# A patch-wise Fourier stage: one product per group in place of two, and a fixed order on three engines

## The chip, the cores and the metric

The kernel runs on one core of one Trainium2 chip. The metric is the device time of one execution in microseconds; the median of three runs before the change is 7702.65 us (7696.43 to 7703.76). Engines are named as in the profile: PE is TensorE (PEld its weight loads), DVE is VectorE, ACT is ScalarE, POOL is GpSimd, SP is SyncE, which here only issues transfers (DMAs).

## The reference

Four layers are applied to an image of 48 channels and 128 x 128 pixels, each on the normalised image and added to it: an attention, a chain of one-dimensional convolutions swept over rows and columns, the patch layer, and a state-space scan. The change lies in the patch layer:

```python
hidden = _conv2d(x, w_hidden, b_hidden)
qkv = _conv2d(hidden, w_dw, b_dw, groups=C6, padding='SAME')
q, k, v = jnp.split(qkv, 3, axis=1)
q_patch = q.reshape(B, C2, hp, wp, PATCH, PATCH)
k_patch = k.reshape(B, C2, hp, wp, PATCH, PATCH)
q_fft = jnp.fft.rfft2(q_patch)
k_fft = jnp.fft.rfft2(k_patch)
out = jnp.fft.irfft2(q_fft * k_fft, s=(PATCH, PATCH))
out = out.reshape(B, C2, H, W)
mu = jnp.mean(out, axis=1, keepdims=True)
var = jnp.var(out, axis=1, keepdims=True)
normed = (out - mu) / jnp.sqrt(var + EPS)
normed = normed * gamma[None, :, None, None] + beta[None, :, None, None]
return _conv2d(v * normed, w_out, b_out)
```

C is 48, C2 is 96, C6 is 288, PATCH is 8. The reshape to patches takes 64 consecutive pixels of a row as one patch of 8 x 8, so a row of 128 pixels holds two patches. Each patch of q is convolved circularly with that of k, the result is normalised over its 96 channels, gated by v, and taken back to 48 channels.

## The kernel before

The four layers run one after the other. `patch_conv` (L696 to L892) works on 32 groups of G = 4 image rows, with pixels on the partitions and channels along the free axis, all in float32. PE does a float32 product as two instructions, so a product in the code is two records in the profile.

The stages of a group:

- `fill` (L759, eight rows, so two groups) writes the normalised rows into the padded image `xp` (the profile's xa; DVE, L93; POOL sets a row of ones, L761), copies 49 channels one row up to partitions 64 and on (L764), fills the partitions that are left with pieces of further taps (L767, two transfers), and puts what does not fit into one of three tiles `rest` (L777, six transfers of 19 partitions x 1038 elements). All nine transfers of a fill are issued by SP. The first three of the six serve even rows, the others odd rows.
- `convolve` (L782, half a group at a time) makes the 3 x 3 convolution of two rows: three products a row over 128 partitions ("columns", L795, tile pc), then one over the 57 partitions of `rest` ("remainder", L804), and ACT copies pc to qkv (L812).
- `keys` and `queries` take the Fourier transform by products with the table `fm` (L821, tile f). f has one PSUM buffer of two banks. Of the keys ACT makes two copies, kn (L836) and kx with real and imaginary part exchanged (two instructions, L839). Of the queries DVE multiplies both with f (L845, twice).
- `back` takes the inverse transform of the two products with the table `gm`, adding them up in PSUM (L852, tile po, kn then kx). DVE takes the mean and subtracts it (L860 to L863), ACT squares (L865), DVE sums (L867), ACT takes the root (L869), DVE divides (L870, L871), and POOL applies gamma, beta and v (L872 to L874).
- `turn` transposes y on PE (L881) and ACT copies it (L883). `leave` makes the last product (L887); DVE adds it to the image (L891) and takes statistics for the next layer (L892).

The groups are pipelined by hand in the loop at the end of `patch_conv`: iteration g holds the convolution of group g, keys and queries of g-1, back of g-2, and turn and leave of g-3, and a fill ahead of them in every second iteration.

The text is put in an order for each engine by a scheduler, which may move instructions of the text past each other where no dependency forbids it. A call through `InOrder` (L32) instead adds to each instruction a dependency on the one before it through the same object, with no semaphore, so that this engine keeps to the order of the text. In the profile all instructions that are issued through `InOrder` carry the helper's line, L48. Before the change `patch_conv` has no such order. Transfers issued by SP and by ACT signal on eight semaphores that are used in turn, and one that takes a semaphore again waits for the transfer that had it before; so no more than eight are open at once.

After the stage, `image_out` (L1525) stores the image for the scan in eight transfers on SP (L1531), and the scan begins.

Of the kernel before, what the change touches and what calls it, by code (L numbers as in the profile page):

```python
# [26 lines left out]
C = 48  # L27
# [668 lines left out]
def patch_conv(ctx, tc, xq, other, const, ins):  # L696

    nc = tc.nc
    ident = const["ident"]
# [21 lines left out]
    gm = wp.tile([128, 2, 64], F32, name="gm")  # L721
    nc.sync.dma_start(gm.rearrange("p f n -> p (f n)"), ins["c_gm"])
# [36 lines left out]
    def fill(r):  # L759
        inside = xp[0:64, 1 + r : 1 + RN + r, 1 : W + 1]  # L760
        nc.gpsimd.memset(inside[32:64], 1.0)  # L761
        normalise(nc, inside[0:C], rows(xq[0:C, r * W : (r + RN) * W]), stats)
        new = slice(r + 1, r + 1 + RN)
        nc.sync.dma_start(xp[64 : 64 + K1, r : r + RN, :], xp[0:K1, new, :])  # L764
        lo, hi = max(r - 1, 0), H if r + RN == H else r - 1 + RN
        for n in range(2):
            nc.sync.dma_start(  # L767
                xp[64 * n + K1 : 64 * n + 64, lo:hi, :],
                xp[M * n : M * n + M, lo + 2 : hi + 2, :],
            )  # L770
        e = rests[r // RN % 3].rearrange("c h w -> c (h w)")
        size = KR // 3
        long = RN * SP - 2
        for n in range(2):
            for dx in range(3):
                at = 64 * n + size * dx
                nc.sync.dma_start(  # L777
                    e[at : at + size, 0:long],
                    flat[2 * M : K1, (r + 1) * SP + dx : (r + 1) * SP + dx + long],
                )  # L780

    qkv, ks, prod, ys, yts = {}, {}, {}, {}, {}  # L782

    def convolve(g, half):

        if half == 0:
            qkv[g] = vp.tile([128, G, C6], F32, name="qkv")
        r0 = g * G + 2 * half  # L790
        pc = [ps_c.tile([128, C6], F32, name="pc") for _ in range(2)]
        last = r0 + 2 == H
        for i in range(2):
            for dx in range(3):
                nc.tensor.matmul(  # L795
                    pc[i],
                    lhsT=xp[:, r0 + i, dx : dx + W],
                    rhs=wt[:, dx, :],
                    start=(dx == 0),
                    stop=(dx == 2 and i == 1 and last),  # L800
                )
        for i in range(1 if last else 2):
            at = 64 * i
            nc.tensor.matmul(  # L804
                pc[i],
                lhsT=rest(r0 + i)[at : at + KR],
                rhs=wt[at : at + KR, 3, :],
                start=False,
                stop=True,
            )  # L810
        for i in range(2):
            nc.scalar.copy(qkv[g][:, 2 * half + i, :], pc[i])  # L812

    def dft(g, at):


        p = ps_f.tile([128, 2, CH], F32, name="f")
        for patch in range(2):
            here = slice(64 * patch, 64 * patch + 64)
            for part in range(2):  # L820
                nc.tensor.matmul(  # L821
                    p[64 * part : 64 * part + 64, patch, 0 : G * C2].rearrange(
                        "f (r c) -> f r c", c=C2
                    ),
                    lhsT=fm[here, part, :],
                    rhs=qkv[g][here, :, at : at + C2],
                    start=True,
                    stop=True,
                )
        return p[:, :, 0 : G * C2]  # L830

    def keys(g):

        p = dft(g, C2)
        ks[g] = [sp.tile([128, 2, G * C2], F32, name=n) for n in ("kn", "kx")]
        nc.scalar.copy(ks[g][0], p)  # L836
        for part in range(2):
            here, there = (slice(64 * n, 64 * n + 64) for n in (part, 1 - part))
            nc.scalar.copy(ks[g][1][here], p[there])  # L839

    def queries(g):
        p = dft(g, 0)
        prod[g] = ks.pop(g)
        for k in prod[g]:
            nc.vector.tensor_mul(k, p, k)  # L845

    def back(g):

        po = ps_o.tile([128, G, C2], F32, name="po")
        for i, t in enumerate(prod.pop(g)):  # L850
            for patch in range(2):
                nc.tensor.matmul(  # L852
                    po[64 * patch : 64 * patch + 64].rearrange("p r c -> p (r c)"),
                    lhsT=gm[:, i, :],
                    rhs=t[:, patch],
                    start=(i == 0),
                    stop=(i == 1),
                )
        mu = sp.tile([128, G], F32, name="mu")
        nc.vector.tensor_reduce(mu, po, AX.X, ALU.add)  # L860
        nc.vector.tensor_scalar_mul(mu, mu, 1.0 / C2)
        y = sp.tile([128, G, C2], F32, name="y")
        nc.vector.tensor_sub(y, po, over_channels(mu))  # L863
        sq = sp.tile([128, G, C2], F32, name="sq")
        nc.scalar.activation(sq, y, AF.Square)  # L865
        var = sp.tile([128, G], F32, name="var")
        nc.vector.tensor_reduce(var, sq, AX.X, ALU.add)  # L867
        nc.vector.tensor_scalar(var, var, 1.0 / C2, 1e-5, ALU.mult, ALU.add)
        nc.scalar.activation(var, var, AF.Sqrt)  # L869
        nc.vector.reciprocal(var, var)  # L870
        nc.vector.tensor_mul(y, y, over_channels(var))  # L871
        nc.gpsimd.tensor_mul(y, y, over_rows(gamma))  # L872
        nc.gpsimd.tensor_add(y, y, over_rows(beta))
        nc.gpsimd.tensor_mul(y, y, qkv.pop(g)[:, :, 2 * C2 :])  # L874
        ys[g] = y

    def turn(g):
        y = ys.pop(g)
        pt = ps_o.tile([C2, G, 128], F32, name="po")
        for r in range(G):  # L880
            nc.tensor.transpose(pt[:, r, :], y[:, r, :], ident)  # L881
        yts[g] = sp.tile([C2, G, 128], F32, name="yt")
        nc.scalar.copy(yts[g], pt)  # L883

    def leave(g):
        pw = ps_o.tile([C, CH], F32, name="po")
        nc.tensor.matmul(  # L887
# [650 lines left out]
def constants():  # L1538
# [7 lines left out]
    p, f = np.arange(64), np.arange(40)  # L1546
    turn = 2.0 * np.pi / 8.0 * (np.outer(p // 8, f // 5) + np.outer(p % 8, f % 5))
    weight = np.where((f % 5 == 0) | (f % 5 == 4), 1.0, 2.0) / 64.0
    fm = np.zeros((2, 64, 2, 64))
    fm[:, :, 0, :40] = np.cos(turn)  # L1550
    fm[:, :, 1, :40] = -np.sin(turn)
    gm = np.zeros((2, 64, 2, 64))
    gm[0, :40, 0] = (np.cos(turn) * weight).T
    gm[1, :40, 0] = -gm[0, :40, 0]
    gm[:, :40, 1] = (-np.sin(turn) * weight).T
# [7 lines left out]
        "c_gm": gm.reshape(128, 128),  # L1563
# [135 lines left out]
```

## Time and profile before

| what | value |
|---|---|
| median of three runs | 7702.65 us |
| the profiled execution | 7707.8 us, of which span 7706.0 us |
| PE busy, whole span | 6227.8 us (81%) |
| the patch stage, 4514 to 4961 us: PE, DVE, ACT, POOL busy | 404.13, 194.29, 161.83, 97.28 of 447 us |
| mean granted PE clock in the stage | 0.94 of full |
| first columns of the stage | 4523.09 us |
| start of the scan's part after 4961 us: PE, DVE, POOL busy | 1472.89, 2603.67, 2578.60 of 2745 us |

Times in the profile count from the start of the span. A line of the timeline gives start, busy time, engine, line of the code, operation, the tile written and the tiles read, partitions x columns, the shape and the number of instructions merged, and in brackets the idle time before it and what ended it. A line by stretches gives, for each engine, the busy time and the number of instructions, then the granted PE clock, the mean busy share of the core's 16 DMA engines, and the GB/s that they moved. The records of PE overlap, since matmuls are pipelined, so the distance between two starts tells the price of one, not the duration listed.

### The profile page before, as it was taken

Reading aid. Unit: us, or ns where it says so; the run is one execution under the profiler, and the core shown is the slowest. Engines: PE = TensorE matmul, PEld = TensorE weight load, DVE = VectorE, ACT = ScalarE, POOL = GpSimd, SP = SyncE. Lnnn points to the kernel's source line nnn. Section 1 sums busy time; section 2 is a strip of 40 time slices with the busy share of each in tenths; the row PEclk is TensorE's granted clock in tenths of the full one; section 3 lists DMA queues with packets and bytes.
Section 4 is the critical chain, followed back from the end, with each engine's and each line's share of the span. In section 5 each row is a group of like instructions: output and inputs, shape, how many; then the busy total and the mean of one; then the engine's idle time right before and its main releaser. Section 6 shows DMA issues by size and latency. Waiting matters only on the chain. (4 is left out here: it accounts for less than half of the span.)

```text
span 7706.0 us, 203399 instructions
## 1 busy us (share of the span) xinstructions
PE 6227.8 (81%) x93872; PEld 3159.4 (41%) x93872; DVE 3377.0 (44%) x2467; ACT 4455.4 (58%) x4928; POOL 2793.0 (36%) x573
## 2 busy tenths in 40 slices
PE   7999999999999999999888889745545554554555
PEld 2333333333333333333377755334434343434444
DVE  8300000000000000000022234489999999999998
ACT  2566666666666666666624014366666666666665
POOL 1000000000000000000000122289999999999998
PEclk9999999999999999999999999867767767676676
DMA  5000000000000000000000011166556656666775
GB/s 76 10 3 3 3 2 3 3 3 2 3 3 3 2 3 3 2 3 3 6 1 17 1 31 48 23 166 166 158 160 161 157 161 154 163 157 161 180 180 148
DMA packets 167597, 488.84 MB, mean 63 GB/s; under 512 B 33440, under 2 KB 51968, under 8 KB 163984
## 3 DMA queue, kind: packets, MB, share of 16 engines
q1 hardware_dynamic: 160704, 470.30, 24.3%
q8 instruction: 737, 12.08, 0.7%
q10 hardware_dynamic: 6032, 5.44, 0.3%
q14 instruction: 124, 1.02, 0.0%
HBM read 428.86 MB, written 22.02 MB: 59 GB/s over the span
## 5 line engine op out<-in xcount | busy, mean ns | idle before, releaser
L48 ACT ACTIVATE e<-s,absT 128x1024 f32<-128x1024 f32 x2048 | 2277.3, 1114 | 1217.9 <-PE s L48 1217.9
L1459 POOL TENSOR_TENSOR h<-du,bt 128x3072 f32<-128x3072 f32 (+1 forms) x386 | 2559.5, 6666 | 102.7 <-DMA du<-rep 70.2
L48 PE MATMUL s<-xa,xb 49*64 49x512 f32 x16384 | 2128.4, 589 | 10.6 <-DVE xb L266 10.6
L48 PE MATMUL acc<-e,xb 64*64 64x512 f32 x16384 | 2125.0, 588 | 0.0
L1466 DVE TENSOR_TENSOR_SCAN h<-dA,carry,h 128x1024 f32<-128x1024 f32 x864 | 1940.7, 2329 | 48.9 <-ACT dA L48 32.9
L48 ACT ACTIVATE dA<-dt,a 128x1024 f32<-128x1024 f32 x1152 | 1287.2, 1118 | 864.0 <-DVE h L1466 854.5
L48 PE MATMUL y<-h,cw 128*32 128x48 f32 x49152 | 899.2, 246 | 949.0 <-issue 511.9
L361 DVE TENSOR_TENSOR osum<-o 128x512 f32<-128x512 f32 x32 | 22.2, 692 | 3114.8 <-ACT o L48 3114.8
L593 POOL MEMSET xa<- 48x128 f32 x1 | 0.3, 326 | 3561.0 <-PE acc L48 3561.0
L48 PEld LDWEIGHTS y<-h,cw 128*32 128x32 f32 x49152 | 809.9, 140 | 1072.3 <-issue 661.8
L48 PEld LDWEIGHTS s<-xa,xb 49*64 49x64 f32 x16384 | 626.3, 132 | 1151.2 <-issue 615.6
L48 PEld LDWEIGHTS acc<-e,xb 64*64 64x64 f32 x16384 | 628.6, 132 | 1133.7 <-issue 1111.2
L1466 DVE TENSOR_TENSOR_SCAN h<-dA,h 128x1024 f32<-128x1024 f32 x288 | 636.1, 2272 | 44.1 <-ACT dA L48 33.6
L48 PE MATMUL yz<-ev,sel 128*8 128x48 f32 x4096 | 192.9, 260 | 277.2 <-ACT ev L48 273.3
L48 PEld LDWEIGHTS yz<-ev,sel 128*8 128x8 f32 x4096 | 162.5, 106 | 334.9 <-ACT ev L48 308.7
L657 PE MATMUL p<-xb,w 112*112 112x129 f32 x1524 | 235.7, 291 | 42.2 <-DVE xb L48 42.1
L657 PE MATMUL p<-xa,w 112*112 112x129 f32 x1524 | 233.5, 289 | 41.8 <-DVE xa L48 41.8
L678 POOL TENSOR_TENSOR xb<-xb,xa 48x2048 f32<-48x2048 f32 (+2 forms) x10 | 44.6, 4464 | 563.0 <-DVE xa L48 563.0
L657 PEld LDWEIGHTS p<-xb,w 112*112 112x112 f32 x1524 | 183.7, 178 | 93.9 <-DVE xb L48 93.9
L640 ACT COPY xa<-xb 48x128 f32<-48x128 f32 x256 | 107.4, 419 | 196.6 <-issue 138.1
L657 PEld LDWEIGHTS p<-xa,w 112*112 112x112 f32 x1524 | 181.8, 177 | 93.3 <-DVE xa L48 93.3
L369 DVE RECIPROCAL rec<-y 48x512 f32<-48x512 f32 x32 | 107.1, 3348 | 257.5 <-ACT y L48 257.5
(187 smaller groups left out, 3602.4 us busy)
## 6 DMA issues: line engine op xcount, KB each, us to landing
du<-rep SPq DMA_DIRECT2D x768, 256.0 KB
dt<-rep SPq DMA_DIRECT2D x768, 256.0 KB
rest<-xa SPq DMA_DIRECT2D x96, 77.0 KB
rest<-band SPq DMA_DIRECT2D x48, 129.9 KB
rep<-dd SPq DMA_DIRECT2D x24, 192.0 KB
yd<-ys ACTq DMA_DIRECT2D x256, 12.0 KB
band<-band SPq DMA_DIRECT2D x8, 414.4 KB
xa<-xa SPq DMA_DIRECT2D x16, 199.1 KB
```

The source lines that it names most:

```text
L48: ins = method(*args, **kwargs).ins
L361: nc.vector.tensor_add(self.o, o[:, 0], o[:, 1])
L369: nc.vector.reciprocal(rec, y[64 : 64 + C])
L593: nc.gpsimd.memset(b[64:K, lines, E + W - 1 : E + W], 0.0)
L640: nc.scalar.copy(u[at : at + C, :, y], t[0:C, E + h, E : E + W])
L657: nc.tensor.matmul(p, lhsT=w[0:K, which, i, :], rhs=state[0:K, 2 * i : 2 * i + L], start=False, stop=(i == 2),)
L678: nc.gpsimd.tensor_add(xr, xr, u[0:C, x : x + xr.shape[2], E : E + H].rearrange("c w h -> c h w"),)
L1459: nc.gpsimd.tensor_mul(h[:, p, ks], du.unsqueeze(1).to_broadcast([128, ks.stop - ks.start, LC]), r["bt"][:, ks],)
L1466: nc.vector.tensor_tensor_scan(h[:, p, k, :], dA, h[:, p, k, :], carry[:, i, k : k + 1] if ci else 0.0, ALU.mult, ALU.add,)
```

## The change

It has five parts.

1. The transforms of a patch are packed into 64 real numbers (30 pairs and four that are real by themselves; before, 40 real and 40 imaginary parts of which some repeat). `fm` now holds two forms, one with the halves exchanged. Keys are transformed once with both forms, on the two halves of the partitions, and queries twice with the first, so one product of 128 partitions takes the place of kn and kx. ACT makes one copy of the keys, DVE one multiplication, and `back` has two products (four records) instead of four.
2. `convolve` is split: `columns` makes all twelve products over 128 partitions of a group, `others` the four remainders and the four copies. Between them stands the `turn` of an older group.
3. PE, ACT and DVE issue through `InOrder`, so they follow the text: columns g, turn g-3, others g, keys g-1, back g-2, leave g-3, queries g-1.
4. `back` ends with the square; the rest of the normalisation and the gating is `gate`, placed after `leave`, and ahead of the queries' product and of the image's statistics (`count`) on DVE.
5. The six `rest` transfers of the first fill are issued by ACT instead of SP; the later fills are written at the end of an iteration instead of the start.

```diff
--- before.py
+++ after.py
@@ -696,6 +696,7 @@
 def patch_conv(ctx, tc, xq, other, const, ins):
 
     nc = tc.nc
+    act, pe, dve = (InOrder(tc, e) for e in (nc.scalar, nc.tensor, nc.vector))
     ident = const["ident"]
     C2, C6 = 2 * C, 6 * C
     G = 4
@@ -718,8 +719,8 @@
 
     fm = wp.tile([128, 2, 64], F32, name="fm")
     nc.sync.dma_start(fm.rearrange("p f n -> p (f n)"), ins["c_fm"])
-    gm = wp.tile([128, 2, 64], F32, name="gm")
-    nc.sync.dma_start(gm.rearrange("p f n -> p (f n)"), ins["c_gm"])
+    gm = wp.tile([128, 64], F32, name="gm")
+    nc.sync.dma_start(gm, ins["c_gm"])
     gamma = wp.tile([128, C2], F32, name="gamma")
     nc.scalar.dma_start(gamma, ins["l2_gamma"].to_broadcast([128, C2]))
     beta = wp.tile([128, C2], F32, name="beta")
@@ -756,7 +757,7 @@
 
         return rests[(y + 1) // RN % 3][:, (y + 1) % RN, 0:W]
 
-    def fill(r):
+    def fill(r, queue=nc.sync):
         inside = xp[0:64, 1 + r : 1 + RN + r, 1 : W + 1]
         nc.gpsimd.memset(inside[32:64], 1.0)
         normalise(nc, inside[0:C], rows(xq[0:C, r * W : (r + RN) * W]), stats)
@@ -774,55 +775,60 @@
         for n in range(2):
             for dx in range(3):
                 at = 64 * n + size * dx
-                nc.sync.dma_start(
+                queue.dma_start(
                     e[at : at + size, 0:long],
                     flat[2 * M : K1, (r + 1) * SP + dx : (r + 1) * SP + dx + long],
                 )
 
-    qkv, ks, prod, ys, yts = {}, {}, {}, {}, {}
-
-    def convolve(g, half):
-
-
-
-        if half == 0:
-            qkv[g] = vp.tile([128, G, C6], F32, name="qkv")
-        r0 = g * G + 2 * half
-        pc = [ps_c.tile([128, C6], F32, name="pc") for _ in range(2)]
-        last = r0 + 2 == H
-        for i in range(2):
+    pcs, qkv, prod, lns, ys, yts = {}, {}, {}, {}, {}, {}
+
+    def columns(g):
+
+
+
+        pcs[g] = [ps_c.tile([128, C6], F32, name="pc") for _ in range(G)]
+        for i, pc in enumerate(pcs[g]):
             for dx in range(3):
-                nc.tensor.matmul(
-                    pc[i],
-                    lhsT=xp[:, r0 + i, dx : dx + W],
+                pe.matmul(
+                    pc,
+                    lhsT=xp[:, g * G + i, dx : dx + W],
                     rhs=wt[:, dx, :],
                     start=(dx == 0),
-                    stop=(dx == 2 and i == 1 and last),
+                    stop=(dx == 2 and outside(g, i)),
                 )
-        for i in range(1 if last else 2):
-            at = 64 * i
-            nc.tensor.matmul(
-                pc[i],
-                lhsT=rest(r0 + i)[at : at + KR],
-                rhs=wt[at : at + KR, 3, :],
-                start=False,
-                stop=True,
-            )
-        for i in range(2):
-            nc.scalar.copy(qkv[g][:, 2 * half + i, :], pc[i])
-
-    def dft(g, at):
+
+    def outside(g, i):
+
+        return g * G + i + 1 == H
+
+    def others(g):
+
+        qkv[g] = vp.tile([128, G, C6], F32, name="qkv")
+        for i, pc in enumerate(pcs[g]):
+            at = 64 * (i % 2)
+            if not outside(g, i):
+                pe.matmul(
+                    pc,
+                    lhsT=rest(g * G + i)[at : at + KR],
+                    rhs=wt[at : at + KR, 3, :],
+                    start=False,
+                    stop=True,
+                )
+        for i, pc in enumerate(pcs.pop(g)):
+            act.copy(qkv[g][:, i, :], pc)
+
+    def dft(g, at, forms):
 
 
         p = ps_f.tile([128, 2, CH], F32, name="f")
         for patch in range(2):
             here = slice(64 * patch, 64 * patch + 64)
-            for part in range(2):
-                nc.tensor.matmul(
-                    p[64 * part : 64 * part + 64, patch, 0 : G * C2].rearrange(
+            for n, form in enumerate(forms):
+                pe.matmul(
+                    p[64 * n : 64 * n + 64, patch, 0 : G * C2].rearrange(
                         "f (r c) -> f r c", c=C2
                     ),
-                    lhsT=fm[here, part, :],
+                    lhsT=fm[here, form, :],
                     rhs=qkv[g][here, :, at : at + C2],
                     start=True,
                     stop=True,
@@ -831,44 +837,43 @@
 
     def keys(g):
 
-        p = dft(g, C2)
-        ks[g] = [sp.tile([128, 2, G * C2], F32, name=n) for n in ("kn", "kx")]
-        nc.scalar.copy(ks[g][0], p)
-        for part in range(2):
-            here, there = (slice(64 * n, 64 * n + 64) for n in (part, 1 - part))
-            nc.scalar.copy(ks[g][1][here], p[there])
+        p = dft(g, C2, (0, 1))
+        prod[g] = sp.tile([128, 2, G * C2], F32, name="k")
+        act.copy(prod[g], p)
 
     def queries(g):
-        p = dft(g, 0)
-        prod[g] = ks.pop(g)
-        for k in prod[g]:
-            nc.vector.tensor_mul(k, p, k)
+        p = dft(g, 0, (0, 0))
+        dve.tensor_mul(prod[g], p, prod[g])
 
     def back(g):
 
         po = ps_o.tile([128, G, C2], F32, name="po")
-        for i, t in enumerate(prod.pop(g)):
-            for patch in range(2):
-                nc.tensor.matmul(
-                    po[64 * patch : 64 * patch + 64].rearrange("p r c -> p (r c)"),
-                    lhsT=gm[:, i, :],
-                    rhs=t[:, patch],
-                    start=(i == 0),
-                    stop=(i == 1),
-                )
+        t = prod.pop(g)
+        for patch in range(2):
+            pe.matmul(
+                po[64 * patch : 64 * patch + 64].rearrange("p r c -> p (r c)"),
+                lhsT=gm,
+                rhs=t[:, patch],
+                start=True,
+                stop=True,
+            )
         mu = sp.tile([128, G], F32, name="mu")
-        nc.vector.tensor_reduce(mu, po, AX.X, ALU.add)
-        nc.vector.tensor_scalar_mul(mu, mu, 1.0 / C2)
+        dve.tensor_reduce(mu, po, AX.X, ALU.add)
+        dve.tensor_scalar_mul(mu, mu, 1.0 / C2)
         y = sp.tile([128, G, C2], F32, name="y")
-        nc.vector.tensor_sub(y, po, over_channels(mu))
+        dve.tensor_sub(y, po, over_channels(mu))
         sq = sp.tile([128, G, C2], F32, name="sq")
-        nc.scalar.activation(sq, y, AF.Square)
+        act.activation(sq, y, AF.Square)
+        lns[g] = y, sq
+
+    def gate(g):
+        y, sq = lns.pop(g)
         var = sp.tile([128, G], F32, name="var")
-        nc.vector.tensor_reduce(var, sq, AX.X, ALU.add)
-        nc.vector.tensor_scalar(var, var, 1.0 / C2, 1e-5, ALU.mult, ALU.add)
-        nc.scalar.activation(var, var, AF.Sqrt)
-        nc.vector.reciprocal(var, var)
-        nc.vector.tensor_mul(y, y, over_channels(var))
+        dve.tensor_reduce(var, sq, AX.X, ALU.add)
+        dve.tensor_scalar(var, var, 1.0 / C2, 1e-5, ALU.mult, ALU.add)
+        act.activation(var, var, AF.Sqrt)
+        dve.reciprocal(var, var)
+        dve.tensor_mul(y, y, over_channels(var))
         nc.gpsimd.tensor_mul(y, y, over_rows(gamma))
         nc.gpsimd.tensor_add(y, y, over_rows(beta))
         nc.gpsimd.tensor_mul(y, y, qkv.pop(g)[:, :, 2 * C2 :])
@@ -878,39 +883,46 @@
         y = ys.pop(g)
         pt = ps_o.tile([C2, G, 128], F32, name="po")
         for r in range(G):
-            nc.tensor.transpose(pt[:, r, :], y[:, r, :], ident)
+            pe.transpose(pt[:, r, :], y[:, r, :], ident)
         yts[g] = sp.tile([C2, G, 128], F32, name="yt")
-        nc.scalar.copy(yts[g], pt)
+        act.copy(yts[g], pt)
 
     def leave(g):
         pw = ps_o.tile([C, CH], F32, name="po")
-        nc.tensor.matmul(
+        pe.matmul(
             pw, lhsT=wout, rhs=yts.pop(g).rearrange("c r w -> c (r w)"), start=True, stop=True
         )
         xc = xq[0:C, g * CH : (g + 1) * CH]
-        nc.vector.scalar_tensor_tensor(xc, pw, bout, xc, ALU.add, ALU.add)
-        nc.vector.bn_stats(const["st"][:, g, :], xc)
+        dve.scalar_tensor_tensor(xc, pw, bout, xc, ALU.add, ALU.add)
+
+    def count(g):
+        dve.bn_stats(const["st"][:, g, :], xq[0:C, g * CH : (g + 1) * CH])
 
     NG = H // G
-    fill(0)
+    fill(0, act)
     fill(RN)
     for g in range(NG + 3):
-        if g % (RN // G) == 0 and (g // (RN // G) + 2) * RN < H:
-            fill((g // (RN // G) + 2) * RN)
+
         if g < NG:
-            convolve(g, 0)
+            columns(g)
+        if g >= 3:
+            turn(g - 3)
+        if g < NG:
+            others(g)
         if 0 <= g - 1 < NG:
             keys(g - 1)
-        if g < NG:
-            convolve(g, 1)
-        if g >= 3:
-            turn(g - 3)
-        if 0 <= g - 1 < NG:
-            queries(g - 1)
         if 0 <= g - 2 < NG:
             back(g - 2)
         if g >= 3:
             leave(g - 3)
+        if 0 <= g - 2 < NG:
+            gate(g - 2)
+        if 0 <= g - 1 < NG:
+            queries(g - 1)
+        if g >= 3:
+            count(g - 3)
+        if g % (RN // G) == 0 and (g // (RN // G) + 2) * RN < H:
+            fill((g // (RN // G) + 2) * RN)
@@ -1543,24 +1555,29 @@
-    p, f = np.arange(64), np.arange(40)
...
-    gm = np.zeros((2, 64, 2, 64))
...
+    rows_, cols_ = np.divmod(np.arange(64), 8)
+    once = [(0, 0), (0, 4), (4, 0), (4, 4)]
+    twice = [(a, b) for b in (1, 2, 3) for a in range(8)] + [(a, b) for b in (0, 4) for a in (1, 2, 3)]
...
+    fm[:, :, 0, 0:30] = np.cos(turn[:30]).T
+    fm[:, :, 0, 32:62] = -np.sin(turn[:30]).T
+    fm[:, :, 0, [30, 31, 62, 63]] = np.cos(turn[30:]).T
+    fm[:, :, 1, :32], fm[:, :, 1, 32:] = fm[:, :, 0, 32:], fm[:, :, 0, :32]
+    gm = np.zeros((2, 64, 64))
...
-        "c_gm": gm.reshape(128, 128),
+        "c_gm": gm.reshape(128, 64),
```

More of the change, by code (lines that the diff above doesn't have):

```diff
@@ L1542, in constants @@
     blk[:64, :64] = blk[64:, 64:] = 1.0
-    p, f = np.arange(64), np.arange(40)
-    turn = 2.0 * np.pi / 8.0 * (np.outer(p // 8, f // 5) + np.outer(p % 8, f % 5))
-    weight = np.where((f % 5 == 0) | (f % 5 == 4), 1.0, 2.0) / 64.0
-    fm = np.zeros((2, 64, 2, 64))
-    fm[:, :, 0, :40] = np.cos(turn)
-    fm[:, :, 1, :40] = -np.sin(turn)
-    gm = np.zeros((2, 64, 2, 64))
-    gm[0, :40, 0] = (np.cos(turn) * weight).T
-    gm[1, :40, 0] = -gm[0, :40, 0]
-    gm[:, :40, 1] = (-np.sin(turn) * weight).T
+    rows_, cols_ = np.divmod(np.arange(64), 8)
+    once = [(0, 0), (0, 4), (4, 0), (4, 4)]
+    twice = [(a, b) for b in (1, 2, 3) for a in range(8)] + [(a, b) for b in (0, 4) for a in (1, 2, 3)]
+    angle = 2.0 * np.pi / 8.0
+    turn = angle * np.array([a * rows_ + b * cols_ for a, b in twice + once])
+    fm = np.zeros((2, 64, 2, 64))
+    fm[:, :, 0, 0:30] = np.cos(turn[:30]).T
[3 more added lines that the diff above has]
+    gm = np.zeros((2, 64, 64))
+    gm[0, 0:30] = 2.0 / 64.0 * np.cos(turn[:30])
+    gm[0, 32:62] = -gm[0, 0:30]
+    gm[0, [30, 31, 62, 63]] = np.cos(turn[30:]) / 64.0
+    gm[1, 0:30] = gm[1, 32:62] = -2.0 / 64.0 * np.sin(turn[:30])
     tables = {
```

## The prediction

> **What bounds the kernel now.** I read the page first, to place the stage that is edited; then the busy time by stretches; then PE's timeline of one group of image rows in the steady part; then the start and the end of the stage.
>
> ```profile
> span 7706.0 us, 203399 instructions
> ...
> PE   7999999999999999999888889745545554554555
> ```
>
> A slice is 192.65 us. The patch stage runs from 4514 to 4961 us, slices 23 to 25. The scan after it, 2745 us, has PE 54% busy, DVE 95% and POOL 94%; the edit does not touch it, so what the stage saves arrives at the end unchanged.
>
> ```profile
> core 0: us, PE busy (x) PEld busy (x) DVE busy (x) ACT busy (x) POOL busy (x), PEclk, DMA share, GB/s
> 4536.00:4538.00 2.00, 2.00 (x5) 1.43 (x5) 0.00 (x0) 0.00 (x0) 0.00 (x0) 0.50 0.07 27
> ...
> 4640.00:4680.00 40.00, 40.00 (x205) 22.14 (x204) 16.72 (x33) 17.51 (x34) 11.64 (x12) 1.00 0.21 60
> ```
>
> In the steady part PE is busy 40.00 of 40 us at full clock, while DVE, ACT and POOL stay under half. PE's work is the bound there. The first row belongs to the start, below.
>
> ```profile
> 4707.46 3.18 PE L795 MATMUL pc<-wt,xa 128*128 128x288 f32 x12
> 4710.56 0.76 PE L804 MATMUL pc<-wt,rest 57*128 57x288 f32 x4
> ...
> 4715.85 0.64 PE L881 MATMUL po<-ident,y 128*96 128x128 f32 x4
> 4716.42 0.88 PE L821 MATMUL f<-qkv,fm 64*64 64x384 f32 x8
> 4717.23 0.87 PE L852 MATMUL po<-kn,gm 128*64 128x384 f32 x4
> 4717.92 0.81 PE L852 MATMUL po<-kx,gm 128*64 128x384 f32 x4
> 4718.57 1.02 PE L887 MATMUL po<-yt,wout 96*48 96x512 f32 x2
> 4719.52 3.18 PE L795 MATMUL pc<-wt,xa 128*128 128x288 f32 x12
> ```
>
> These are lines of one group, start time first, no gap between them: 4719.52 - 4707.46 = 12.06 us. Costs are differences of starts, since the listed durations overlap.
>
> **The steady group, part by part.**
> (1) The pair kx is gone: 4718.57 - 4717.92 = 0.65 us. The kn pair keeps 0.69 (4717.23 to 4717.92).
> (2) The 24 column records stand in one run instead of two of 12. A run of 12 takes 3.10 us to the next start; a run of 8 (4544.14 to 4546.28) takes 2.14; so a record is 0.24 and a run has a fixed 0.20. One run: 24 x 0.2425 + 0.20 = 6.02 instead of 6.22 (twice 3.11 in the neighbouring groups).
> (3) The remainder products (L804) keep 2 x 0.69 = 1.38, the transforms (L821) 0.81 each, transposes 0.57, the exit 0.95. Queries move behind the exit, at the same price.
> New group: 6.02 + 0.57 + 1.38 + 0.81 + 0.69 + 0.95 + 0.81 = **11.23 us, 0.83 less.**
> (4) ACT loses the two kx copies (2 x 0.80) and DVE one product (0.95). I count nothing: ACT then has 4 x 0.40 + 0.80 + 0.52 + 0.20 + 0.58 = 3.7 us per group and DVE about 5.1, both covered by 11.23 of PE. Without that cover they would be worth 1.6 and 0.95 per group.
> (5) Keys and queries share one PSUM buffer, so queries wait for ACT's copy (0.80). Back and exit lie between, 0.69 + 0.95 = 1.64, so it is hidden from the third iteration on.
> (6) Fill moves to the end of an iteration. The compiled order shows the memsets on POOL, the sixteen normalisations on DVE and the transfers on SP in the places they had, except for the first fill's six, which go to ACT's queue. On SP the stores of the result now stand ahead of some later fills; each needs a row group that has left long before the fill's buffer comes free. Nothing counted. The smaller gm table (32 KB less) is loaded well ahead.
>
> **The wait that the fixed order adds.** PE must now run the transposes of group g-2 straight after the columns of the next group, ahead of remainders, keys, back, exit and queries; all of these stand behind it if POOL is late, and behind them ACT's copies and DVE's products. So I followed one group from its back product to its transposes.
>
> ```profile
> 4903.16 0.55 DVE L867 TENSOR_REDUCE var<-sq 128x4 f32<-128x384 f32 x1 [0.65 <-ACT sq L865]
> ...
> 4905.11 1.00 POOL L872 TENSOR_TENSOR y<-y,gamma 128x384 f32<-128x384 f32 x1 [8.92 <-DVE y L871]
> ...
> 4948.23 0.56 DVE L860 TENSOR_REDUCE mu<-po 128x4 f32<-128x384 f32 x1 [7.22 <-PE po L852]
> ...
> 4949.74 0.52 ACT L865 ACTIVATE sq<-y 128x384 f32<-128x384 f32 x1 [3.65 <-DVE y L863]
> ...
> 4956.16 1.09 PE L881 MATMUL po<-ident,y 128*96 128x128 f32 x4 [6.28 <-POOL y L874]
> ```
>
> Mean to square: 4949.74 - 4948.23 = 1.51. Square to the sum of squares 0.56 where nothing delays it (4938.19 to 4938.75). Sum of squares to POOL: 4905.11 - 4903.16 = 1.95. POOL's three: 1.07 + 1.07 + 0.99, and 0.06 to PE. With the 0.87 of the back product and 0.06 to DVE: 0.93 + 1.51 + 0.56 + 1.95 + 3.19 = 8.14 us. PE meanwhile has back, exit, queries and columns: 0.69 + 0.95 + 0.81 + 6.02 = 8.47. **Spare 0.33 us; no wait.** The sum holds the exit's addition on DVE, which ends as the squares do. The statistics, which cost the chain up to 0.6 us in the old drain, now stand behind the product.
>
> **The start.** PE begins at 4523.09 and waits 5.22 us (to 4533.88), 5.45 (to 4562.84) and 1.74 (to 4582.49), each for the rest tiles.
>
> ```profile
> 4533.88 1.29 PE L804 MATMUL pc<-wt,rest 57*128 57x288 f32 x2 [5.22 <-DMA rest<-xa]
> ...
> 4562.84 2.25 PE L804 MATMUL pc<-wt,rest 57*128 57x288 f32 x4 [5.45 <-DMA rest<-xa]
> ```
>
> While only rest transfers run, the DMA share is 0.06 to 0.07, one engine in sixteen, at 25 to 27 GB/s: 77 KB take about 3.05 us. Up to eight were open at once and none took a second engine, so I take it that their shape chooses the engine and that the six on ACT's queue, of the same shape, use the same one. Then twelve rest transfers and the two fills' other shares, 12 x 3.05 + 3 = 39.6 us from about 4520.5, end at 4560 to 4561, whoever issues them: only 2 us sooner than 4562.84. With fixed order PE has by then done columns and remainders of group 0 and columns 1, and waits for row 7. From 4560.5: the last remainder, keys and queries at a slow clock 4.0, then columns 2 (6.02), remainders, keys, back, queries (3.7), columns 3 (6.02), its transposes at back + 8.14 (1.2 later), remainders, keys, back, exit, queries (4.7): columns 4 start near 4586.1. Before, 4586.81. Gain 0.7. Were the two queues served on two engines, no wait would bind and columns 4 could start at 4566, a gain of 21; were ACT's transfers served last, 10 later than I say.
> The Trainium skill, "DMA: Bandwidth & Descriptors", section "Why a DMA increments its semaphore by 16 and not by 1", gives a rule that speaks against the second queue: a copy uses as many engines as the largest number up to 16 that divides its slowest dimension, the lowest-numbered ones, so 19 partitions get one engine and both queues the same one. By that rule the start gains 0.7, against 21 if queues were independent. No row of this trace has both queues at such transfers.
>
> **The end.** Before, from the last group's columns at 4912.55 to the statistics' total at 4961.51: 48.96. After: columns 6.02; then transposes, remainders, keys 2.76; chain 8.14; at the slow clock that follows waiting, transposes 1.02, keys 1.49; back, 0.65 longer, and chain 8.79; transposes 1.02; chain 8.79, and 0.36 for a slow exit ahead of the sum; then 5.35 as before (4956.16 to 4961.51): 43.7. Gain 5.2.
>
> **Sum.** 27 groups (4 to 30) x 0.83 = 22.4, start 0.7, end 5.2: 28.3 us. The profiled execution took 7707.8 us (span 7706.0 and 1.8 around it): 7679.5. The median of the runs is 5.1 under it, so **7675 us**.
>
> **Rivals.**
> (a) The transposes wait a little in every group, 0.2 to 0.6 us: the spare is only 0.33. For it: each of ten handovers is uncertain by some hundredths. Time 7680 to 7692.
> (b) Slower: the same wait grown large. Back follows the transposes in order, so a group cannot be shorter than 2.76 + chain. The old time returns when that reaches 11.23 + 28.3 / 27 = 12.28, a chain of 9.5 instead of 8.14. For it: the old drain ran at 11.55 and 11.83 us per group, and POOL now works beside DVE's product. Against it: that drain had slow clock and statistics in the chain; and POOL's 4929.59 ran beside DVE's product in 1.00 us, with 1.003 the maximum of all 32. At 13.0 per group, a chain of 10.2: 7675 + 27 x 1.77 = 7723.
> (c) Independent queues: 28.3 + 20.5 = 49 less, 7654. Against it: the share of one sixteenth.
> (d) Rest transfers cannot keep pace and set the group. One fill needs about 19.5 us (SP's first transfers of consecutive fills start at 4566.40 and 4585.42) against 22.5 for two groups; it would have to grow by 3. Time at 24 per fill: near 7696.
>
> **How the numbers follow.** Main case 0.67 (7667 to 7682), (a) 0.13, (b) 0.10, (c) 0.05, (d) 0.05. The range 7666 to 7692 holds the main case, (a), and ACT's transfers served last (7685). A difference under 0.2%, 15 us, can't be told from none. Faster takes the main case, (c) and two thirds of (a): 0.81; the same (d), the rest of (a) and a third of (b), where the growth stops short: 0.12; slower the rest of (b): 0.07.
>
> **What would show it.** Groups 11.2 us apart on PE, with kx gone and 24 column records in a run; no wait for POOL's y ahead of the transposes until the drain; two waits for rest tiles, ending near 4560; columns 4 near 4586; the statistics' total near 4933. Wrong if the groups lie 11.6 or more apart with PE idle ahead of the transposes, or if the start is over by 4570.

## The result and the profile after

| what | before | after |
|---|---|---|
| median of six runs | 7701.84 us | 7666.91 us |
| the profiled execution | 7707.8 us | 7668.22 us |
| the patch stage, from the statistics' total that opens it to the one that ends it | 446.81 us | 415.38 us |

The ratio of the medians is 0.9956 (95% interval 0.9943 to 0.9969): 34.9 us less, where 27.6 were forecast. The time lies inside the range (7666 to 7692), 0.9 us above its lower edge.

The two profiled executions differ by 39.6 us, and not all of it is the change. Ahead of the stage the same instructions took 3.9 us less, behind it 4.3 us less. Over the eleven profiles of this study the part ahead of the stage varies between 4507.8 and 4516.5 us and the part behind it between 2728.2 and 2747.1, whatever was changed in the stage. So the stage's own length is the finer measure: 31.4 us less. It is used below for each experiment, beside the medians.

A line of the page after, and two rows by stretches (columns as before: length, busy time and count of PE, PEld, DVE, ACT and POOL, granted PE clock, DMA share, GB/s):

```profile
span 7666.4 us, 202951 instructions
```

```profile
4680.00:4698.00 18.00, 15.21 (x68) 7.81 (x61) 6.23 (x14) 4.04 (x9) 3.00 (x3) 0.81 0.26 65
...
4709.00:4731.00 22.00, 22.00 (x118) 13.18 (x117) 9.94 (x21) 6.76 (x16) 6.00 (x6) 1.00 0.16 43
```

The last row is the steady part: PE is busy all the time at full clock, as before, so it is still the bound. The row above it is a stretch that the kernel before did not have: 18 us with PE idle for almost 3 of them, at a clock of 0.81.

One steady group on PE, to be set against the group shown before:

```profile
4708.45 6.09 PE L48 MATMUL pc<-wt,xa 128*128 128x288 f32 x24
4714.37 0.60 PE L48 MATMUL po<-ident,y 128*96 128x128 f32 x4
4714.90 1.24 PE L48 MATMUL pc<-wt,rest 57*128 57x288 f32 x8
4716.07 0.88 PE L48 MATMUL f<-qkv,fm 64*64 64x384 f32 x8
4716.88 0.87 PE L48 MATMUL po<-k,gm 128*64 128x384 f32 x4
4717.57 1.02 PE L48 MATMUL po<-yt,wout 96*48 96x512 f32 x2
4718.53 0.88 PE L48 MATMUL f<-qkv,fm 64*64 64x384 f32 x8
4719.33 5.84 PE L48 MATMUL pc<-wt,xa 128*128 128x288 f32 x23
```

From columns to columns 4719.33 - 4708.45 = 10.88; over many groups it is 10.89. (The view ends at 4725.00, so the last line counts 23 of 24 records.) The pair kx is gone, and no line waits.

Where the 31.4 us are, by the starts of columns 4 and columns 31 as the marks: start of the stage to columns 4, 71.42 instead of 72.11, 0.7 gained; columns 4 to 31, 300.40 instead of 325.74, 25.3 gained; columns 31 to the end, 43.56 instead of 48.96, 5.4 gained. The middle could have given 27 x (12.064 - 10.89) = 31.7; 6.4 were lost in the one group that the stretch above shows:

```profile
4680.29 6.09 PE L48 MATMUL pc<-wt,xa 128*128 128x288 f32 x24
...
4690.77 1.29 PE L48 MATMUL pc<-wt,rest 57*128 57x288 f32 x2 [2.79 <-DMA rest<-xa]
4691.99 1.56 PE L48 MATMUL f<-qkv,fm 64*64 64x384 f32 x8
...
4697.56 6.09 PE L48 MATMUL pc<-wt,xa 128*128 128x288 f32 x24
```

This group is 4697.56 - 4680.29 = 17.27 us long. Its last remainder waits for a rest tile, and then the products run at a slow clock: a transform's eight records are listed with 1.56 us in place of 0.88, and the granted clock is half:

```profile
4691.00:4694.00 3.00, 3.00 (x12) 0.83 (x14) 0.00 (x0) 0.78 (x2) 0.00 (x0) 0.50 0.66 149
```

From the waiting remainder to the next columns 6.79 us pass, where the steady group needs about 3.55. So about half of the loss is the wait and half what follows it.

The start of the stage:

```profile
4523.17 7.58 PE L48 MATMUL pc<-wt,xa 128*128 128x288 f32 x24 [10.04 <-DMA xa<-xa]
...
4547.23 2.26 PE L48 MATMUL pc<-wt,rest 57*128 57x288 f32 x6 [15.79 <-DMA rest<-xa]
...
4557.46 1.24 PE L48 MATMUL pc<-wt,rest 57*128 57x288 f32 x8
...
4582.23 6.09 PE L48 MATMUL pc<-wt,xa 128*128 128x288 f32 x24
```

The total of the statistics stands at 4510.81, so columns 0 start 12.36 us behind it (before: 8.39). Then comes one long wait for the first fill's odd rows, and group 1's remainders (4557.46) wait for nothing, though only just: in the trace's DMA packets the last of their rest tiles ends at 4557.27.

### The profile page after: what moved, and what is told of

The parts are those of the page before. It is cut to its first block, busy times and chain, and to the rows that moved or that the text cites. A ratio compares the mean times of both kernels' runs of the same rounds, so it can differ in the third digit from the quotient of the medians.

```text
span 7666.4 us, 202951 instructions
## 1 busy us (share of the span) xinstructions
PE 6186.0 (81%) x93744; PEld 3145.7 (41%) x93744; DVE 3353.1 (44%) x2435; ACT 4405.6 (57%) x4864; POOL 2793.6 (36%) x573
## 3 DMA queue, kind: packets, MB, share of 16 engines
q8 instruction: 736, 12.06, 0.7%
q10 hardware_dynamic: 6152, 5.92, 0.3%
## 5 line engine op out<-in xcount | busy, mean ns | idle before, releaser
L1478 DVE TENSOR_TENSOR_SCAN h<-dA,h 128x1024 f32<-128x1024 f32 x288 | 636.1, 2270 | 45.9 <-ACT dA L48 34.9
```

The lines of the kernel that those rows point to most:

```text
L1478: nc.vector.tensor_tensor_scan(h[:, p, k, :], dA, h[:, p, k, :], carry[:, i, k : k + 1] if ci else 0.0, ALU.mult, ALU.add,)
```

## The experiments

Each kernel was timed against the kernel before on the same chip. "Exit" is the first product of `leave` (po<-yt), counted from the total that opens the stage: 71.16 us before, 69.66 after.

### Packing alone

The kernel before, with the packed tables, one copy of the keys, one multiplication and one pair of products; no fixed order, nothing moved.

```diff
-        for i, t in enumerate(prod.pop(g)):
-            for patch in range(2):
...
+        t = prod.pop(g)
+        for patch in range(2):
```

> The kernel before with the packed transforms alone; the scheduler orders as before. Theory (PE's own work sets the group): kx leaves PE, 0.65 us a group, so a group of 12.06 becomes 11.41 and the stage, 446.8 us from one statistics total to the next, becomes 446.8 - 27 x 0.65 - 2.5 for the two slow groups of the drain = 427. Rival 1 (the group is also freed by ACT's and DVE's work): under 422. Rival 2 (transposes wait once the groups are shorter): over 432.

Measured: 7679.51 us, ratio 0.9971 (0.9959 to 0.9982). Stage 426.06, 20.8 us less; groups 11.42 apart, 0.64 less than before, which is the price of the pair kx (0.65). Both are as expected (427 and 11.41), and the two rivals fall. Two columns one group apart:

```profile
4702.07 3.18 PE L795 MATMUL pc<-wt,xa 128*128 128x288 f32 x12
...
4713.49 3.18 PE L795 MATMUL pc<-wt,xa 128*128 128x288 f32 x12
```

### Order alone

The kernel after, with the kernel before's tables, three copies of the keys, two multiplications and both pairs of products.

```diff
-        act.copy(prod[g], p)
+        prod[g] = [sp.tile([128, 2, G * C2], F32, name=n) for n in ("kn", "kx")]
+        act.copy(prod[g][0], p)
+        for part in range(2):
...
+            act.copy(prod[g][1][here], p[there])
```

> The changed kernel with the two products kn and kx put back: order, grouping by shape and place of the fills as changed. Theory: a group of 10.89 + 0.65 = 11.54 us, and no wait for rest tiles in the middle of the stage, since two groups give the fills 23.1 us instead of 21.8; the stage 415.4 + 27 x 0.65 + 2.5 - 6.4 = 429. If grouping by shape is worth nothing and only kx was, the groups are 12.0 and the stage over 440. Rival (ACT's three copies again between keys and queries): PE waits ahead of queries, about 0.5 us a group, stage 443.

Measured: 7699.31 us, ratio 0.9999 (0.9990 to 1.0009). Stage 442.08: only 4.7 us less than before. The theory (11.54 and 429) missed; the rival's wait is there, 0.29 us a group and not 0.5, and the stage is near its 443. The groups are 11.83 apart, 0.94 more than after: 0.65 for the pair and 0.29 more. PE's queries stand behind ACT's three copies, since keys and queries share a PSUM buffer:

```profile
4702.59 0.88 PE L48 MATMUL f<-qkv,fm 64*64 64x384 f32 x8 [0.23 <-ACT kx L48]
```

So in the fixed order the two kx copies were on the path of PE, and taking them away earns 0.29 us a group there. The parts do not simply add: packing alone takes 0.64 from the group, the order alone 0.23 (12.06 - 11.83), both together 1.17 (12.06 - 10.89). The 0.29 is a difference of these numbers; the listed wait of 0.23 is what stands for it in the trace. The start pays too: the exit is at 74.83, 5.2 later than after, with waits of 2.54 and 1.08 us for kx in the first groups.

### The change without the fixed order

```diff
-    act, pe, dve = (InOrder(tc, e) for e in (nc.scalar, nc.tensor, nc.vector))
+    act, pe, dve = nc.scalar, nc.tensor, nc.vector
```

> The changed kernel without the fixed order on the three engines; the scheduler keeps PE's order but puts the queries' product ahead of the variance's scaling and the statistics ahead of the reciprocal on DVE. Theory (the path from back to transposes has a spare of some 0.2 to 0.3 us): the path grows by 0.95 + about 0.4, PE waits about 1.1 us in each group, groups of 12.0, the stage about 445, time about that of the kernel before. Rival (the spare is larger, order on DVE does not matter): groups of 10.9 and stage 415.

Measured: 7682.84 us, ratio 0.9977 (0.9967 to 0.9986). Stage 432.2, groups 11.62 apart, 0.73 more than after (1.1 expected; the rival's 415 is refuted). PE runs the same order of products; DVE and PE show what differs:

```profile
4709.85 0.55 DVE L872 TENSOR_REDUCE var<-sq 128x4 f32<-128x384 f32 x1
4710.32 0.95 DVE L846 TENSOR_TENSOR k<-f,k 128x768 f32<-128x768 f32 x1
...
4711.25 0.68 DVE L899 BATCH_NORM_STATS2 st<-xb 48x6 f32<-48x512 f32 x1
```

```profile
4715.94 0.64 PE L886 MATMUL po<-ident,y 128*96 128x128 f32 x4 [0.54 <-POOL y L879]
```

The scheduler puts the queries' product between the sum of squares and its scaling, and the statistics ahead of the reciprocal. Both places lie in the chain from the back product to the transposes, and PE now waits for POOL in every group.

### The gate behind the queries' product and the statistics

```diff
-        if 0 <= g - 2 < NG:
-            gate(g - 2)
         if 0 <= g - 1 < NG:
             queries(g - 1)
         if g >= 3:
             count(g - 3)
+        if 0 <= g - 2 < NG:
+            gate(g - 2)
```

> The changed kernel with the gate written after the queries' product and the image's statistics, all else equal. Theory: DVE sums the squares 2.0 us later (product when the queries are done, then 0.65 of statistics), PE waits 2.0 less the spare of 0.25, 1.75 us in each group, groups of 12.6, stage about 465: slower than the kernel before by 15 to 20 us. Rival (the place on DVE is nothing, since PE is the bound): 415.

Measured: 7697.17 us, ratio 0.9992 (0.9983 to 1.0002). Stage 445.15, groups 12.03 apart, 1.14 more than after; the expectation (12.6 and 465) was too high: the sum of squares comes 1.38 us later, not 2.0. DVE, and PE's wait:

```profile
4708.49 0.94 DVE L48 TENSOR_TENSOR k<-f,k 128x768 f32<-128x768 f32 x1
...
4709.95 0.53 DVE L48 TENSOR_REDUCE var<-sq 128x4 f32<-128x384 f32 x1
```

```profile
4715.06 0.64 PE L48 MATMUL po<-ident,y 128*96 128x128 f32 x4 [0.94 <-POOL y L879]
```

The sum of squares starts 4.37 us behind the back product (4705.58) in place of 2.99 (4708.98 - 4705.99 after). The chain is 1.38 longer, and 1.38 less the 1.14 that the group grew leaves 0.24: that much the chain had to spare in the kernel after. The place of the gate alone decides over all but 1.7 us of the stage's gain (446.81 - 445.15).

### The first fill's rests back on SP

```diff
-    fill(0, act)
+    fill(0)
```

> The changed kernel with the first fill's six rest transfers back on SP. Theory (all rest transfers are served by the same DMA engine, whichever queue they come from): the columns of group 0 start about 4 us sooner, since nothing of ACT's stands before the first copies, but the last of the first two fills' rest transfers lands at the same time within 2 us, so the first exit product stays 69.7 us after the statistics total within 2 us and the stage at 413 to 418. Rival (the second queue runs beside the first): the start is 10 us or more longer, stage over 425.

Measured: 7663.69 us, ratio 0.9948 (0.9932 to 0.9965). Stage 414.65, the same as after within 0.7. Exit 73.72, 4.1 later than after. The waits of the start:

```profile
4536.39 2.25 PE L48 MATMUL pc<-wt,rest 57*128 57x288 f32 x6 [8.40 <-DMA rest<-xa]
...
4556.23 1.29 PE L48 MATMUL pc<-wt,rest 57*128 57x288 f32 x2 [8.36 <-DMA rest<-xa]
```

The two traces must be compared from the total that opens the stage (4507.80 here, 4510.81 after). Columns 0 start 8.69 us behind it, 3.7 sooner than after, as expected. With one queue the first fill's last tiles come 7.8 us sooner (28.6 behind the total, not 36.4), and those of row 7 at 48.4, where after they are there at 46.7 at the latest. The last DMA packet of the two fills' rests ends at 47.8 here and at 46.5 after. So when the series ends hardly depends on who issues it, as one engine for all of them would have it. It does not fit two engines, for which the rival asked 10 us or more.

The exit was expected within 2 us of after and came 4.1 later. About 1.8 of this is the later tile. The rest follows the wait of 8.36 us: the granted clock is 0.50 from 4557.5 to 4559, a transform's eight records are listed with 1.56 us and the 24 of the next columns with 6.96, in place of 0.88 and 6.09 after, where no such wait stands ahead of them. The 4.1 us that the second queue does earn are spent in the middle: here the group with the late rest tile waits 0.87 us and is 12.47 long, there it waits 2.79, and by the exits it is 16.28 long and the next 11.88.

### Rest transfers cut into 16 and 3 partitions

```diff
-                queue.dma_start(
-                    e[at : at + size, 0:long],
...
+                for lo_, hi_ in ((0, 16), (16, size)):
+                    queue.dma_start(
+                        e[at + lo_ : at + hi_, 0:long],
...
```

> The changed kernel with each rest transfer of 19 partitions issued as two, of 16 and of 3 partitions. Theory (19 partitions go to one DMA engine, 16 to sixteen): a rest transfer takes well under 1 us of the engines instead of 3.05, the waits of 10 and 15.8 us at the start and of 2.8 in the middle go; first exit product at about 50 us instead of 69.7, no group over 11.3, stage about 389, total about 7641. Rival (the queue takes some 3 us for each transfer, whatever its shape): twelve instead of six transfers a fill, groups of 18 us or more, slower than the kernel before.

Measured: 7647.88 us, ratio 0.9926 (0.9909 to 0.9942). Stage 388.1, exit 48.75, no group over 10.98, as expected (389, 50 and 11.3). Start of the stage on PE, and one stretch of it:

```profile
4524.58 8.93 PE L48 MATMUL pc<-wt,xa 128*128 128x288 f32 x24 [7.30 <-DMA xa<-xa]
4533.44 1.24 PE L48 MATMUL pc<-wt,rest 57*128 57x288 f32 x8
```

```profile
4532.00:4534.00 2.00, 2.00 (x11) 1.34 (x11) 0.00 (x0) 0.00 (x0) 0.00 (x0) 1.00 0.40 75
```

No remainder waits any more. In this stretch only cut rests are issued (SP's from 4525.63 on): the DMA share is 0.40 at 75 GB/s, where it was 0.06 to 0.07 at 25 to 27 GB/s with the uncut transfers alone. The start gains 69.66 - 48.75 = 20.9 us by it, though each of the six is now issued twice. The compiled order of SP changed too in the middle, so the other 6.4 us of the stage's 27.3 can come from the cut or from that order. The run with SP held to the text, below, shows that the order is enough; the cut in the old order was not tried.

### The drain in another order

The last keys, both last back products and the last queries are put ahead of the last three groups' transposes.

```diff
+    keys(c)
+    back(b)
+    queries(c)
+    gate(b)
+    back(c)
+    turn(a)
+    leave(a)
+    gate(c)
+    count(a)
...
```

> The changed kernel with another order after the last columns: the last keys, both last back products and the last queries go ahead of the three last transposes, instead of one back product after each. Theory (the drain is three paths of 8 to 9 us one after the other, because PE's fixed order puts each back product behind the transposes before it): two of the three lie beside each other, the drain from last columns to the total falls from 43.6 to about 32, stage about 404. Rival (POOL's three operations and DVE set the drain): 412 or more.

Measured: 7655.01 us, ratio 0.9937 (0.9921 to 0.9954). Stage 407.79 (404 expected); from the last columns to the total 36.4 us in place of 43.6 (32 expected). The last exits follow each other by 14.16, 4.15 and 5.43 us in place of 11.26, 10.10 and 9.55.

```profile
4896.55 0.88 PE L48 MATMUL f<-qkv,fm 64*64 64x384 f32 x8 [3.19 <-DVE k L48]
...
4913.46 1.09 PE L48 MATMUL po<-ident,y 128*96 128x128 f32 x4 [1.67 <-POOL y L879]
```

The chains now overlap: of the waits for POOL only 1.67 us is left. PE waits instead for DVE's product, which still holds the PSUM buffer f; these 3.19 us are of the size of what is missing (3.8), but that they are the cause was not tested. That the drain was bounded by chains standing one after the other is shown.

### SP held to the text as well

This run looks for the cause of the wait in the middle. SP's issues in the kernel before, then after (SPq is its queue):

```profile
4610.41 14.59 SPq L777 DMA_DIRECT2D rest<-xa  x6
4638.84 7.37 SPq L777 DMA_DIRECT2D rest<-xa  x6
4667.47 5.55 SPq L777 DMA_DIRECT2D rest<-xa  x6
```

```profile
4642.01 5.49 SPq L778 DMA_DIRECT2D rest<-xa  x6
4647.54 4.43 SPq L768 DMA_DIRECT2D xa<-xa  x2
4652.07 0.71 SPq L765 DMA_DIRECT2D xa<-xa  x1
4652.82 3.03 SPq L768 DMA_DIRECT2D xa<-xa  x2
4658.59 0.71 SPq L765 DMA_DIRECT2D xa<-xa  x1
4661.91 4.02 SPq L768 DMA_DIRECT2D xa<-xa  x2
4666.04 0.71 SPq L765 DMA_DIRECT2D xa<-xa  x1
4666.79 0.80 SPq L768 DMA_DIRECT2D xa<-xa  x1
4667.70 5.61 SPq L778 DMA_DIRECT2D rest<-xa  x6
```

Fills follow each other by 28.43 and 28.63 us there in the kernel before too, more than its two groups (24.1): six, then eleven first copies of later fills stand between. It had no wait, since PE came later. After, PE comes to this group 15 us sooner by the trace's clock (columns at 4680.29, before at 4586.81 + 9 x 12.064 = 4695.4), and the rests of its fill are issued at the same time (4667.70, before 4667.47). Counted from the total that opens the stage, which stands 3.9 us earlier after, PE comes 11.2 us sooner and the rests are issued 4.1 us later: SP has issued 41 first copies ahead of them, before 35.

```diff
+    sp_queue = InOrder(tc, nc.sync)
...
-        nc.sync.dma_start(xp[64 : 64 + K1, r : r + RN, :], xp[0:K1, new, :])
+        sp_queue.dma_start(xp[64 : 64 + K1, r : r + RN, :], xp[0:K1, new, :])
...
```

> The kernel after, with the transfers of the later fills on SP held to the order of the text too: a fill's three first copies, then its six rests, then the next fill. In the kernel after SP issues the first copies of later fills ahead of the rests of fill 56 (ten copies between the rests at 4642.01 and those at 4667.70), and PE loses 6.4 us there. Theory 1, the copies that ran ahead took the time: the spacing of fills falls to about 20 us, as in the early fills, under two groups (21.78), no group is longer than 11.0, and the stage takes 415.4 - 6.4 = 409. Theory 2, a fill's rests on one engine are too long by themselves beside PE at full speed: a wait for a rest tile of 2 us or more stays in the steady part, and the stage takes 414 or more.

Measured: 7658.1 us, ratio 0.9950 (0.9936 to 0.9963). Stage 408.53 (409 expected), no group over 10.97. SP, and PE at the place:

```profile
4627.75 12.89 SPq L48 DMA_DIRECT2D rest<-xa  x6
4640.69 6.71 SPq L48 DMA_DIRECT2D xa<-xa  x3
4647.51 13.42 SPq L48 DMA_DIRECT2D rest<-xa  x6
```

```profile
4686.74 1.24 PE L48 MATMUL pc<-wt,rest 57*128 57x288 f32 x8
```

Fills lie about 20 us apart, with the uncut transfers on their one engine, and the remainders run together without a wait. The copies that ran ahead were the cause; theory 2 falls. That the fills are now written at the end of an iteration was not tried alone, so its share in the changed order of SP stays open.

### Cut transfers and the other drain together

> The changed kernel with the rest transfers of 16 and 3 partitions and the other order of the drain, together. If both theories hold the savings add, since they lie at the two ends of the stage: stage about 378, total about 7630. If either rival holds, the sum shows only the other.

Measured: 7641.28 us, ratio 0.9912 (0.9895 to 0.9928), stage 381.05. It is the fastest version of this study, ahead of both kernels: 65.8 us less of stage than before, where the change had 31.4. The two gains add up within 0.6 us: 27.3 + 7.6 = 34.9, measured 34.3. Expected were 378 and 7630; the missing 3 us of stage are of the size of what the other drain had missed alone (3.8).

## Why the prediction was right, and where it was not

**The sign and the mechanism were right.** PE's own work bounds the group before and after; the chain stayed just inside its slot, and the changes of PE's work arrived at the end.

**The steady group: 10.89, not 11.23.** The terms against the lines shown: columns 5.92 (6.02), transposes 0.53 (0.57), remainders 1.17 (1.38), keys 0.81, back 0.69, exit 0.96, queries 0.80. The mis-sized term is the remainders: the prediction took a fixed 0.20 us per run of records for the columns, and then kept two runs of remainders, though the change joins those too, eight records in one run. Twice 0.69 less one fixed 0.20 is 1.18. The same rule, applied to each line of the group, would have given 11.03.

**The chain: right.** One group after, from its back product to its transposes:

```profile
4705.99 0.87 PE L48 MATMUL po<-k,gm 128*64 128x384 f32 x4
4706.90 0.56 DVE L48 TENSOR_REDUCE mu<-po 128x4 f32<-128x384 f32 x1 [6.23 <-PE po L48]
...
4708.98 0.55 DVE L48 TENSOR_REDUCE var<-sq 128x4 f32<-128x384 f32 x1
...
4713.08 1.00 POOL L879 TENSOR_TENSOR y<-y,qkv 128x384 f32<-128x384 f32 x1
```

The last of POOL's three ends at 4714.08, and with 0.06 to PE the chain is 8.15 (8.14 forecast). The slot is 4714.37 - 4705.99 = 8.38 (8.47). The spare of 0.23 is the 0.24 that the gate's experiment gave by another way. So rivals (a) and (b) did not occur, though (a) was only a quarter of a microsecond off. Without the fixed order DVE's order brings (a) on, and with the gate last nearly (b): the groups lie 12.03 apart, and almost all of the gain is given back.

**The rest transfers: a rival that came true in one group.** The forecast dismissed (d) with the spacing of early fills, 19.5 us (the two starts that it names lie 19.0 apart). The later fills of the same trace lie 28.4 and 28.6 apart, and it made no use of them. That SP's transfers stay in the places they had held only roughly: six more first copies stand ahead of these rests than before. What had been early enough for PE before was 2.79 us late for a faster PE. The price was 6.4 us, in one group only.

**The two errors cancel.** Twenty-seven groups gave 31.7 in place of 22.4 (9.3 more), the late tile took 6.4 of it: 25.3. That the middle came out within 3 us of the forecast is in part luck, and so is that the time lies inside the range: the run with SP held to the text, which has no late tile, took 7658.1, below the range.

**The start: the sum right, its way wrong.** 0.7 us forecast and 0.7 found; columns 4, forecast near 4586, start at 4582.23 in a trace whose total stands 3.9 us earlier, so at 4586.1 on the forecast's clock. But the waits forecast, two ending near 4560, did not come; there is one of 10.04 for the first copies and one of 15.79 for the first fill's rests. The forecast had the first fill served as early as before; the run with one queue shows that sharing the engine with the second fill is what makes it late. What held is the bound: one engine carries all of it, and the last rest ends at 4557.27, on the forecast's clock 4561.2 (4560 to 4561 forecast). PE, held up by the first fill's tiles, comes to these only 0.2 us later (4557.46); that the two meet there is luck. The Trainium skill, "DMA: Bandwidth & Descriptors", section "Why a DMA increments its semaphore by 16 and not by 1", lets a copy use the largest number of engines up to 16 that divides its slowest dimension; the cut into 16 and 3 agrees with it, a share of 0.40 in place of 0.06.

**The end.** 43.7 forecast, 43.56 measured, with the forecast waits for POOL's y in it:

```profile
4899.18 1.09 PE L48 MATMUL po<-ident,y 128*96 128x128 f32 x4 [5.60 <-POOL y L879]
...
4910.76 1.09 PE L48 MATMUL po<-ident,y 128*96 128x128 f32 x4 [4.92 <-POOL y L879]
...
4920.85 1.09 PE L48 MATMUL po<-ident,y 128*96 128x128 f32 x4 [5.82 <-POOL y L879]
```

From the last columns (4882.63) the three transposes start 16.55, 11.58 and 10.09 us after each other. The forecast's terms make 6.02 + 2.76 + 8.14 = 16.92, then 1.02 + 1.49 + 8.79 = 11.30, then 1.02 + 8.79 + 0.36 = 10.17. The errors (0.37 too much, 0.28 too little, 0.08 too much) nearly cancel.

**The sum.** 28.3 us were forecast for the stage, 31.4 came. By the medians it is 34.9; the other 3.5 are of the size by which the untouched code varies from run to run, and were not forecast.

## What to carry to other kernels

When an engine that is the bound becomes faster, look for every transfer that it meets later in the stage and ask how early each one was, over the whole stage and not in its first rows: part of the gain can be spent on a transfer that was just early enough before. A fixed order on the engines is worth trying where one chain runs through several of them with little to spare: here the place of two instructions on DVE decided over 1.14 us of a group, and the order alone had gained 0.23. And count a fixed price per run wherever equal shapes are joined, not only at the ones that the change names.

## What the runs showed of the hardware

- A transfer of 19 partitions used one DMA engine of sixteen; that was forecast. A cut into 16 and 3 pays although it doubles the issues: share 0.40, and the start of the stage 20.9 us shorter (the expectation of that run had it within 1.3).
- Two queues with such transfers do not go side by side, but they do mix: the first fill's last tiles came 36.4 us behind the total with two queues and 28.6 with one, and the series of both fills ended at 46.5 and 47.8.
- A wait can cost PE more than its length. After 2.79 us of waiting the granted clock was 0.50 (4691 to 4694) and the transform's eight records were listed with 1.56 us in place of 0.88; of the 6.4 us lost about half came after the wait. After 0.87 us of waiting, in the run with one queue, the clock stayed at 1.00 (4712 to 4716) and the eight records took 0.88. Where between the two the limit lies was not measured.
